# Weighted sum of shifted images: bands through DRAM, and x as the stationary operand

## The chip, the cores and the metric

The kernel runs on one core of a Trainium2 chip. The metric is device time in microseconds (us). The core has five engines that run side by side, each with its own list of instructions in order: PE (TensorE, matrix products and transposes), DVE (VectorE), ACT (ScalarE), POOL (GpSimd) and SP (SyncE, which here only issues DMA transfers). PE reads SBUF and writes PSUM, and DVE and ACT empty PSUM. Everything is float32.

## The reference

The input x has 4 images of 256 channels and 64 x 64 pixels. For each image:

```
k    = conv(x, w1, 7x7 taps, dilation 2, padding 6) + b1      # 128 channels
k    = conv(k, w2, 1x1) + b2                                  # 49 channels, one per tap
attn = softmax(k over the 49 taps)
y[c, h, w] = sum over taps (u, v) of attn[u*7+v, h, w] * xpad[c, h + 2u, w + 2v]
```

Then y is whitened: within each group of 64 channels its mean and covariance over all images and pixels are taken, five Newton-Schulz steps give the inverse square root of the covariance, that matrix is applied to the centred y, and a gain and a shift follow.

## The kernel before

Dilation 2 makes each image fall into 4 parity sub-images of 32 x 32 pixels in which the taps are dense. So there are 16 sub-images (`NSUB`), numbered n. A sub-image has 8 chunks (`NCH`) of 128 pixels, each chunk 4 rows of 32. x is held in SBUF as one tile per image and row parity, [128 channels, 2 channel halves, 32 rows, 64 columns]. A sub-image takes every second column of such a tile. Two tiles are held at a time, and `load_x` fetches the next ones during the run.

The two convolutions are one: w1 and w2 are multiplied ahead (L147) to `wf`, 49 outputs per tap. `conv_piece` (L193) issues for each of 49 taps and 2 channel halves two matmuls (L208), one for the upper 16 rows of the sub-image (written to partitions 0 to 48) and one for the lower 16 (partitions 64 to 112). That is 196 matmuls for each sub-image. Rows that a tap takes out of the sub-image are left out, so for taps with u < 3 the upper half's matmuls are shorter, and for u > 3 the lower half's.

`softmax` (L218) adds the bias on ACT (L222), transposes the logits so that a pixel has its 49 values in its partition (L227), takes the maximum, subtracts, and writes the exponentials to `e_abs` with four ACT instructions (L241), each row of a chunk at its own place. The sum and its reciprocal follow on DVE (L243, L247).

For each chunk g, `build_band` (L263) makes the 128 pixels' rows of a banded matrix over the source pixels of the chunks before, at and after it, with seven `copy_predicated` instructions on DVE (L271). `transpose_band` turns it by up to three transposes (L284), and ACT copies the result to SBUF (L291). `transpose_x` makes pixels-by-channels blocks of x (L258, L260). `weighted_sum` (L294) multiplies with the band as the stationary operand and x as the moving one, 256 columns, two or three times for each chunk (L299):

```
nc.tensor.matmul(t[:, :C], a[:, d * P : (d + 1) * P], xT[g + d - 1],
                 start=(d == ds_[0]), stop=(d == ds_[-1]))
```

DVE scales by the reciprocal and subtracts a pivot (L316). `collect` (L325) adds the result's second moments to `sig` (L333, 129 columns, the last a column of ones) and transposes it back to channels by pixels (L336); ACT copies that to the tile `y` of the image (L338).

The order is written out in a loop over chunks: a piece of the next sub-image's conv (an eighth, 24 or 26 matmuls), then x transposes of chunk g+1, the band transposes of g, the weighted sum of g-1, the collection of g-2, and at the end of a sub-image the softmax of the next. A framework sets the semaphores and may move instructions a little against the written order. Tiles named `tp` come from four PSUM tiles used in turn.

At the end stand the whitening matrices (L375 to L437, a chain of small products between PE and DVE) and the last loop (L442): 64 matmuls of 512 columns (L449), each followed by a scaling on ACT or DVE in turn, in place, and 16 stores of 1 MB.

Of the kernel before, what the change touches and what calls it, by code (L numbers as in the profile page):

```python
# [9 lines left out]
I32 = mybir.dt.int32  # L10
# [6 lines left out]
def kernel(  # L17
# [11 lines left out]
    """Dilated 7x7 conv -> 1x1 conv -> softmax over the 49 taps -> weighted sum of  # L29
    the 49 dilated shifts of x -> group whitening (Newton-Schulz) -> affine.  # L30

    Dilation 2 splits an image into 4 parity sub-images of 32x32 in which the taps
    are dense. The two convs are one conv with the weight product (49 outputs, two
    half sub-images side by side in the array's columns). The weighted sum is a
    product with a banded matrix A[source pixel, pixel] that is built per 128
    pixels (4 sub-rows) from the softmax.
    """
# [9 lines left out]
    NCH = SH * SW // P  # L47
    CR = P // SW
    NB = CR + KS - 1
# [7 lines left out]

    const = ctx.enter_context(tc.tile_pool(name="const", bufs=1))
    xpool = ctx.enter_context(tc.tile_pool(name="xp", bufs=2))
    xtpool = ctx.enter_context(tc.tile_pool(name="xtp", bufs=5))  # L60
    work = ctx.enter_context(tc.tile_pool(name="work", bufs=2))
    ps_cv = ctx.enter_context(tc.tile_pool(name="ps_cv", bufs=2, space=bass.MemoryType.PSUM))
    ps_tp = ctx.enter_context(tc.tile_pool(name="ps_tp", bufs=4, space=bass.MemoryType.PSUM))
# [6 lines left out]
    xtiles = {}  # L70

    def load_x(k):
        b, pr = divmod(k, 2)
        t = xpool.tile([P, NCC, SH, W], F32, tag="x", name=f"x_{k}")
        for cc in range(NCC):
            src = x[b, cc * P : (cc + 1) * P].rearrange("c (r two) w -> c r two w", two=2)
            nc.sync.dma_start(t[:, cc], src[:, :, pr, :])
        xtiles[k] = t

# [1 line left out]
    ident = const.tile([P, P], F32, name="ident")  # L81
    make_identity(nc, ident)
    ones = const.tile([P, P], F32, name="ones")
    nc.gpsimd.memset(ones, 1.0)
# [5 lines left out]
    # diag[p, R + w] = 1 where w is the sub-column of pixel p; mask[p, v, w'] = 1  # L90
    # where tap column v takes pixel p to source column w'
# [5 lines left out]
    mask = const.tile([P, KS, SW], I32, name="mask")  # L97
    for v in range(KS):
        nc.vector.tensor_copy(mask[:, v, :], diag[:, KS - 1 - v : KS - 1 - v + SW])

# [28 lines left out]
    with tc.tile_pool(name="w1p", bufs=1) as w1p:  # L129
# [8 lines left out]
        load_x(0)  # L138
        load_x(1)
        TG = 10  # L140
        n = 0
        for cc in range(NCC):
            for t0 in range(0, KT, TG):
# [15 lines left out]
                n += 1  # L159

    ypool = ctx.enter_context(tc.tile_pool(name="yp", bufs=1))
    y = [ypool.tile([P, NCC, H, W], F32, name=f"y_{b}") for b in range(B)]

    # Tiles whose zeros (or ones) stay where they are over the whole run.
    logit = const.tile([P, HALF * SW], F32, name="logit")
    nc.gpsimd.memset(logit, 0.0)
    NE = 2
    e_abs = []
    for k in range(NE):
        et = const.tile([P, NCH, NB, KS], F32, name=f"e_abs{k}")  # L170
        nc.gpsimd.memset(et, 0.0)
        e_abs.append(et)
    NA = 2
    at_buf = []
    for k in range(NA):
        a = const.tile([P, 3 * CR, SW], F32, name=f"at{k}")
        nc.gpsimd.memset(a, 0.0)
        at_buf.append(a)
    NY = 3
# [5 lines left out]
    pivot = const.tile([P, C], F32, name="pivot")  # L185

    sig = [ps_sg.tile([P, P + 1], F32, name=f"sig{cc}") for cc in range(NCC)]

# [4 lines left out]
    def conv_piece(n, part, parts):  # L193
        """Part of the conv of sub-image n: rows of half h in partitions 64 h."""
        k, pc = divmod(n, 2)
        xt = xtiles[k]
# [19 lines left out]
    rsum = {}  # L216

    def softmax(n):  # L218
# [7 lines left out]
        for i in range(NI):  # L226
# [7 lines left out]
        d = work.tile([P, NI, 2, KT], F32, tag="d", name=f"d_{n}", bufs=1)  # L234
        nc.vector.tensor_tensor(
            d, lt[:, :, :, :KT], mx.unsqueeze(3).to_broadcast([P, NI, 2, KT]), ALU.subtract
        )
        e = e_abs[n % NE].rearrange("p (h i) a v -> p i h (a v)", h=2)
        for j in range(CR):
            q = slice(j * SW, (j + 1) * SW)  # L240
            nc.scalar.activation(e[q, :, :, j * KS : j * KS + KT], d[q], AF.Exp)  # L241
        s = work.tile([P, NCH], F32, tag="s", name=f"s_{n}")
        nc.vector.tensor_reduce(  # L243
            s, e_abs[n % NE].rearrange("p i a v -> p i (a v)"), AX.X, ALU.add
        )
        rs = work.tile([P, NCH], F32, tag="rs", name=f"rs_{n}", bufs=3)
        nc.vector.reciprocal(rs, s)  # L247
        rsum[n] = rs

    xT = {}  # L250

    def transpose_x(g):
        n, i = divmod(g, NCH)
        k, pc = divmod(n, 2)
        t = tp()
        for cc in range(NCC):
            src = xtiles[k][:, cc, i * CR : (i + 1) * CR, bass.ds(pc, SW, 2)]
            nc.tensor.transpose(t[:, cc * P : (cc + 1) * P], src, ident)  # L258
        xt = xtpool.tile([P, C], F32, tag="xT", name=f"xT_{g}")
        nc.scalar.copy(xt, t[:, :C])  # L260
        xT[g] = xt

    def build_band(g):  # L263
        """Transposed band of chunk g: row p holds the softmax terms of pixel p at
        its source pixels, over the source rows of chunks i-1, i, i+1."""
        n, i = divmod(g, NCH)
        a = at_buf[g % NA]
        e = e_abs[n % NE]
        shape = [P, NB, SW]
        for v in range(KS):  # L270
            nc.vector.copy_predicated(  # L271
                a[:, 1 : 1 + NB, :],
                mask[:, v, :].unsqueeze(1).to_broadcast(shape),
                e[:, i, :, v].unsqueeze(2).to_broadcast(shape),
            )

    bands = {}

    def transpose_band(g):
        i = g % NCH  # L280
        ds_ = [d for d in range(3) if 0 <= i + d - 1 < NCH]
        t = tp()
        for d in ds_:
            nc.tensor.transpose(  # L284
                t[:, d * P : (d + 1) * P],
                at_buf[g % NA][:, d * CR : (d + 1) * CR, :].rearrange("p r w -> p (r w)"),
                ident,
            )
        a = work.tile([P, 3 * P], F32, tag="band", name=f"band_{g}")
        cs = slice(ds_[0] * P, (ds_[-1] + 1) * P)  # L290
        nc.scalar.copy(a[:, cs], t[:, cs])  # L291
        bands[g] = (a, ds_)

    def weighted_sum(g):  # L294
        n, i = divmod(g, NCH)
        a, ds_ = bands.pop(g)
        t = tp()
        for d in ds_:
            nc.tensor.matmul(  # L299
                t[:, :C],  # L300
                a[:, d * P : (d + 1) * P],
                xT[g + d - 1],
                start=(d == ds_[0]),
                stop=(d == ds_[-1]),
            )
        xT.pop(g - 1, None)
# [43 lines left out]
    for g in range(NG + 2):  # L350
        n, i = divmod(g, NCH)
        if g < NG and n + 1 < NSUB:
            conv_piece(n + 1, i, NCH)
# [87 lines left out]
    n = 0  # L441
# [50 lines left out]
```

## Time and profile before

| | |
|---|---|
| median of 3 runs | 1907.37 us (1906.34 to 1908.09) |
| span of the profiled execution | 1905.9 us (first to last instruction; the page gives no other time of it) |
| granted PE clock, mean | 0.980 |
| softmax of sub-image 2 to softmax of sub-image 3 (L227) | 254.57 to 362.57 us |
| conv of the first sub-image ends | 148.1 us |
| conv of the last sub-image ends | 1764.1 us |
| first matmul of whitening (L380) | 1804.04 us |
| first matmul of the last loop (L449) | 1842.80 us |

A line of a timeline or of a group names the engine, the source line, the operation, the tiles (output <- inputs) and the shape, and "x" the number of records. PEld is PE's loading of the stationary operand, which overlaps the products. A float32 matmul leaves two records, a transpose one. Ends of matmuls are modelled and overlap, so the spacing of starts tells the cost. A line of a stretch has the busy time of PE, PEld, DVE, ACT and POOL, each with its number of records, then the granted PE clock, the share of DMA time and the GB/s. A DMA line has the number of issues, the size of each, and the median time from issue to landing in us.

### The profile page before, as it was taken

How to read it: one execution, taken by the hardware profiler on the slowest of the kernel's cores; microseconds unless marked ns; L12 is line 12 of the kernel's file. 1: busy time of each engine (PE TensorE's matmuls, PEld its weight loads, DVE VectorE, ACT ScalarE, POOL GpSimd, SP SyncE). 2: the span in 40 equal slices, each digit the busy share in tenths (PEclk: the TensorE clock that was granted, in tenths of full speed). 3: DMA queues.
4: the chain of work that ended last, by engine and by line, in shares of the span. 5: the costliest groups of instructions: out<-in, count | busy, mean ns of one | idle time of the engine just before them, and what ended most of it. 6: DMA issues, size and time to landing. Idle time of an engine off the chain costs nothing.

```text
span 1905.9 us, 20030 instructions
## 1 busy us (share of the span) xinstructions
PE 1859.7 (98%) x8809; PEld 941.5 (49%) x8809; DVE 562.4 (30%) x1204; ACT 243.1 (13%) x649; POOL 4.7 (0%) x21
## 2 busy tenths in 40 slices
PE   7999999999999999999999999999999999999678
PEld 6544454444545454444554545444544444454543
DVE  0004232322324232322323323231423323231734
ACT  0001010101001010101111111101111111110314
POOL 0000000000000000000000000000000000000000
PEclk9899999999999999999999999999999999999869
DMA  8000000200020000200011000200002000000017
GB/s 224 1 0 1 1 1 1 45 0 1 1 38 7 1 0 1 45 1 1 1 23 22 1 1 1 45 0 1 1 9 37 1 0 1 1 1 1 1 53 300
DMA packets 69358, 41.29 MB, mean 22 GB/s; under 512 B 66919, under 2 KB 66968, under 8 KB 66968
## 3 DMA queue, kind: packets, MB, share of 16 engines
q1 hardware_dynamic: 68984, 33.58, 7.3%
q10 hardware_dynamic: 288, 6.42, 0.8%
q8 instruction: 70, 1.15, 0.3%
q14 instruction: 16, 0.13, 0.0%
HBM read 23.23 MB, written 16.78 MB: 21 GB/s over the span
## 4 chain that ended last, share of the span: by engine, by line
PE 97%; DVE 2%; DMA 1%; issue 0%; ACT 0%; SPq 0%
PE cv L208 73%; PE tp L299 8%; PE tp L449 3%; PE sig L333 3%; PE tp L258 3%; PE tp L147 2%; PE tp L284 2%; PE tp L336 1%; DVE at L271 1%; DMA b_sb<-in_L_conv_b_dram 1%; PE tp L414 0%; PE tp L410 0%; PE tp L406 0%; PE tp L227 0%; DVE P L417 0%
## 5 line engine op out<-in xcount | busy, mean ns | idle before, releaser
L208 PE MATMUL cv<-x,wf 128*49 128x480 f32 (+14 forms) x6272 | 1401.9, 580 | 0.0
L208 PEld LDWEIGHTS cv<-x,wf 128*49 128x49 f32 x6272 | 556.9, 123 | 752.3 <-issue 652.2
L271 DVE COPY_PREDICATED at<-mask,e_abs 128x320 f32<-128x320 int32 x896 | 444.1, 519 | 725.9 <-PE tp L284 709.5
L260 ACT COPY xT<-tp 128x256 f32<-128x256 f32 x128 | 47.4, 370 | 1086.0 <-PE tp L258 1086.0
L299 PE MATMUL tp<-xT,band 128*128 128x256 f32 x704 | 175.1, 383 | 0.0
L316 DVE SCALAR_TENSOR_TENSOR yt<-tp,rs,pivot 128x256 f32<-128x256 f32 x128 | 60.9, 476 | 366.9 <-PE tp L299 366.8
L299 PEld LDWEIGHTS tp<-xT,band 128*128 128x128 f32 x704 | 124.8, 192 | 12.2 <-ACT y L338 0.4
L333 PE MATMUL sig<-yt 128*128 128x129 f32 x512 | 92.1, 276 | 0.1
L258 PEld LDWEIGHTS tp<-ident,x 128*128 128x128 f32 x256 | 40.6, 207 | 101.6 <-issue 101.6
L333 PEld LDWEIGHTS sig<-yt 128*128 128x128 f32 x512 | 87.1, 192 | 7.0 <-DVE yt L316 0.5
L338 ACT COPY y<-tp 128x128 f32<-128x128 f32 x256 | 56.6, 278 | 159.1 <-PE tp L336 159.1
L284 PE MATMUL tp<-ident,at 128*128 128x128 f32 x352 | 60.1, 275 | 11.3 <-DVE at L271 11.3
L336 PE MATMUL tp<-ident,yt 128*128 128x128 f32 x256 | 69.5, 274 | 0.0
L258 PE MATMUL tp<-ident,x 128*128 128x128 f32 x256 | 64.1, 332 | 0.0
L291 ACT COPY band<-tp 128x384 f32<-128x384 f32 (+1 forms) x128 | 57.8, 451 | 15.4 <-PE tp L284 13.6
L449 PE MATMUL tp<-y,P 128*128 128x512 f32 x128 | 57.5, 612 | 0.0
L222 ACT ACTIVATE logit<-cv,bias 49x512 f32<-49x512 f32 x32 | 21.8, 682 | 252.3 <-PE cv L208 251.9
L284 PEld LDWEIGHTS tp<-ident,at 128*128 128x128 f32 x352 | 43.9, 146 | 12.4 <-issue 12.4
L147 PEld LDWEIGHTS tp<-w2T,w 128*128 128x128 f32 x196 | 43.2, 313 | 1.0 <-issue 1.0
L147 PE MATMUL tp<-w2T,w 128*128 128x49 f32 x196 | 43.4, 418 | 0.0
L449 PEld LDWEIGHTS tp<-y,P 128*128 128x128 f32 x128 | 25.2, 198 | 31.5 <-issue 31.5
L233 DVE TENSOR_REDUCE mx<-tp 128x8 f32<-128x392 f32 x16 | 9.1, 566 | 99.7 <-PE tp L227 99.7
(77 smaller groups left out, 236.5 us busy)
## 6 DMA issues: line engine op xcount, KB each, us to landing
x<-in_x_dram SPq DMA_DIRECT2D x16, 1024.0 KB, 11.2
out_dram<-y SPq DMA_DIRECT2D x16, 1024.0 KB, 3.8
w<-in_L_conv_w_dram ACTq DMA_DIRECT2D x2, 3136.0 KB
gain_sb<-in_L_conv_weight_dram SPq DMA_DIRECT2D x2, 0.5 KB, 17.9
shift_sb<-in_L_conv_bias_dram SPq DMA_DIRECT2D x2, 0.5 KB, 17.6
b_sb<-in_L_conv_b_dram SPq DMA_DIRECT2D x2, 0.2 KB
w_sb<-in_L_conv_w_dram SPq DMA_DIRECT2D x1, 24.5 KB
b_sb<-in_L_conv_b_dram SPq DMA_DIRECT2D x1, 0.5 KB
```

The costliest lines, as they stand in the source:

```text
L147: nc.tensor.matmul(t[:, k * KT : (k + 1) * KT], w1_sb[cc][:, :, t0 + k], w2T[:, :KT], start=True, stop=True,)
L208: nc.tensor.matmul(ps[h * HB : h * HB + KT, r0 - h * HALF : r1 - h * HALF, c0:c1], wf[:, cc, u * KS + v, :], xt[:, cc, r0 + du : r1 + du, ...
L258: nc.tensor.transpose(t[:, cc * P : (cc + 1) * P], src, ident)
L271: nc.vector.copy_predicated(a[:, 1 : 1 + NB, :], mask[:, v, :].unsqueeze(1).to_broadcast(shape), e[:, i, :, v].unsqueeze(2).to_broadcast(s ...
L284: nc.tensor.transpose(t[:, d * P : (d + 1) * P], at_buf[g % NA][:, d * CR : (d + 1) * CR, :].rearrange("p r w -> p (r w)"), ident,)
L291: nc.scalar.copy(a[:, cs], t[:, cs])
L299: nc.tensor.matmul(t[:, :C], a[:, d * P : (d + 1) * P], xT[g + d - 1], start=(d == ds_[0]), stop=(d == ds_[-1]),)
L316: nc.vector.scalar_tensor_tensor(yt_buf[g % NY][:, :, :P], t[:, :C].rearrange("p (a c) -> p a c", a=NCC), r, pivot.rearrange("p (a c) -> p ...
L333: nc.tensor.matmul(sig[cc], yt[:, cc, :P], yt[:, cc, :], start=(g == 0), stop=(g == last))
L336: nc.tensor.transpose(t[:, cc * P : (cc + 1) * P], yt[:, cc, :P], ident)
L338: nc.scalar.copy(y[b][:, cc, bass.ds(2 * i * CR + pr, CR, 2), bass.ds(pc, SW, 2)], t[:, cc * P : (cc + 1) * P].rearrange("p (r w) -> p r w ...
L449: nc.tensor.matmul(t, wm[cc], yf[:, k : k + NT], start=True, stop=True)
```

## The change

The band of a whole sub-image is now made at once by a copy through DRAM. DVE writes the normalised softmax values to a tile `zt`, at the same place in every partition and with zeros around them. SP stores it to DRAM with a row pitch of ZL+1 and loads it back with a pitch of ZL, so that each partition's values come back shifted by its own number. The masked reciprocal `rm` removes taps that leave the row.

The weighted sum goes by source block in place of by chunk: `make_block(n, m)` transposes block m of x and the band's rows that touch it; x's block is the stationary operand and the band the moving one, and the products of up to three blocks add up in a PSUM tile of a half sub-image, channels by pixels. As a block reaches 3 rows over its edges, the rows that are new and those that were written before are separate matmuls. The result, minus a pivot, is written by ACT into x's own tile in place of the sub-image's x, so the separate `y` tiles go. All eight x tiles are loaded at the start, the last six behind the product of w1 and w2. `collect` then transposes y to pixels by channels, copies it on DVE, and adds the second moments. The last loop writes to three buffers of 512 KB in place of working in place, with 32 stores. `ps_tp` has three tiles in place of four, and the y product has one pair of PSUM banks. The numbers of lines below are not those of the kernel before.

```diff
+    dram = ctx.enter_context(tc.tile_pool(name="dram", bufs=2, space=bass.MemoryType.DRAM))
-    ps_tp = ctx.enter_context(tc.tile_pool(name="ps_tp", bufs=4, space=bass.MemoryType.PSUM))
+    ps_tp = ctx.enter_context(tc.tile_pool(name="ps_tp", bufs=3, space=bass.MemoryType.PSUM))
+    ps_y = ctx.enter_context(tc.tile_pool(name="ps_y", bufs=1, space=bass.MemoryType.PSUM))
...
+    for k in range(2, 2 * B):
+        load_x(x27, k)
+    nc.vector.tensor_reduce(
+        pivot, slots[0].rearrange("p a r w -> p a (r w)")[:, :, :npix], AX.X, ALU.add
+    )
...
 def softmax(n):   # after the maximum is subtracted
+        nc.scalar.activation(d, d, AF.Exp)
+        nc.vector.tensor_reduce(s, d, AX.X, ALU.add)
+        nc.vector.reciprocal(s, s)
+        nc.vector.tensor_tensor(rm, s.unsqueeze(2).to_broadcast([P, NCH, KS]),
+            cmask.unsqueeze(1).to_broadcast([P, NCH, KS]), ALU.mult)
+        nc.vector.tensor_tensor(
+            zt[:, P : P + NCH * BR * SW].rearrange("p (i a w) -> p i a w", i=NCH, w=SW)[
+                :, :, :KS, :KS],
+            d.rearrange("p i (u v) -> p i u v", u=KS),
+            rm.unsqueeze(2).to_broadcast([P, NCH, KS, KS]), ALU.mult)
+        skew = dram.tile([P * (ZL + 1)], F32, tag="skew", name=f"skew_{n}")
+        nc.sync.dma_start(skew.rearrange("(p l) -> p l", l=ZL + 1)[:, :ZL], zt)
+        src = skew[: P * ZL].rearrange("(p l) -> p l", l=ZL)
+        nc.sync.dma_start(
+            band[:, : (NCH - 1) * BP, :].rearrange("p (i a) w -> p i (a w)", a=BP)[
+                :, :, : BR * SW],
+            src[:, z0 : z0 + n7].rearrange("p (i f) -> p i f", f=BR * SW))
+        nc.sync.dma_start(band[...last rows...], src[:, z0 + n7 : z0 + n7 + (BR - R) * SW])
...
+    def make_block(n, m):
+        t = tp()
+        for cc in range(NCC):
+            nc.tensor.transpose(t[:, cc * P : (cc + 1) * P],
+                xt[:, cc, CR * m : CR * (m + 1), bass.ds(pc, SW, 2)], ident)
+        nc.scalar.copy(xb, t[:, :C])
+        t = tp()
+        for i in range(i0, min(NCH, m + 2)):
+            a0 = BP * i + CR * (m - i) + R
+            nc.tensor.transpose(t[:, (i - i0) * P : (i - i0 + 1) * P],
+                band[:, a0 : a0 + CR, :].rearrange("p r w -> p (r w)"), ident)
+        nc.vector.tensor_copy(bb[:, :nw], t[:, b0 : b0 + nw])
+    def weighted_sum(n, half, m):
+        for cc in range(NCC):
+            for q0, q1 in ((r0, done), (done, r1)):
+                if q0 < q1:
+                    nc.tensor.matmul(
+                        ps[:, cc, q0 - half * HALF : q1 - half * HALF, :],
+                        xb[:, cc * P : (cc + 1) * P],
+                        bb[:, (q0 - w0) * SW : (q1 - w0) * SW],
+                        start=(m == first), stop=(m == last), skip_group_check=True)
+    def store_y(n, half):
+        for cc in range(NCC):
+            nc.scalar.activation(
+                yt[:, cc, half * HALF : (half + 1) * HALF, bass.ds(pc, SW, 2)],
+                ps[:, cc], AF.Identity, bias=pivot[:, cc : cc + 1])
+    def collect(n, half):
+        for i in range(half * NCH // 2, (half + 1) * NCH // 2):
+            t = tp()
+            for cc in range(NCC):
+                nc.tensor.transpose(t[:, cc * P : (cc + 1) * P],
+                    yt[:, cc, CR * i : CR * (i + 1), bass.ds(pc, SW, 2)], ident)
+            yb = yt_buf[count[0] % NY]      # NY = 2; L369 is the copy below
+            nc.vector.tensor_copy(yb[:, :, :P], t[:, :C].rearrange("p (a c) -> p a c", a=NCC))
+            for cc in range(NCC):
+                nc.tensor.matmul(sig[:, cc], yb[:, cc, :P], yb[:, cc, :], ...)
...
+    for n in range(NSUB + 1):
+        steps = [      # mb = make_block, ws = weighted_sum of sub-image n
+            [lambda: collect(n - 1, 1)] if n else [],
+            [mb(0), mb(1)],
+            [ws(0, 0), mb(2), ws(0, 1), mb(3)],
+            [ws(0, 2), mb(4), ws(0, 3), mb(5), ws(0, 4), lambda: store_y(n, 0)],
+            [mb(6), ws(1, 3), ws(1, 4)],
+            [mb(7), ws(1, 5), ws(1, 6)],
+            [lambda: collect(n, 0)],
+            [ws(1, 7), lambda: store_y(n, 1)],
+        ]
+        for part, do in enumerate(steps):
+            if on and n + 1 < NSUB:
+                conv_piece(n + 1, part, NCH)
+            ...
+            for f in do:
+                f()
+        if n + 1 < NSUB:
+            softmax(n + 1)
...
 # last loop
+                st = ring.tile([P, TR, 2, W], F32, tag="out", name=f"out_{b}_{cc}_{q}", bufs=3)
+                for pr in range(2):
+                    nc.tensor.matmul(t, wm[cc], slots[2 * b + pr][:, cc, q * TR : (q + 1) * TR, :]...)
+                    # scaled by ACT (even) or DVE (odd) into st[:, :, pr, :]
+                nc.sync.dma_start(out[b, cc * P : (cc + 1) * P, 2 * q * TR : 2 * (q + 1) * TR, :],
+                    st.rearrange("p r two w -> p (r two) w"))
```

## The prediction

> **What bounds the kernel now.** I read the page's shares first, then the chain of waits, then stretches of one sub-image each, then PE's timeline inside one stretch.
>
> ```profile
> PE 1859.7 (98%) x8809; PEld 941.5 (49%) x8809; DVE 562.4 (30%) x1204; ACT 243.1 (13%) x649; POOL 4.7 (0%) x21
> ...
> PEclk9899999999999999999999999999999999999869
> ...
> PE 97%; DVE 2%; DMA 1%; issue 0%; ACT 0%; SPq 0%
> ```
>
> PE is the chain; DVE, which loses most work by this change, is 2% of it. So only what PE issues, and what makes PE wait, counts.
>
> ```profile
> 254.57:362.57 108.00, 108.00 (x529) 53.63 (x528) 32.40 (x69) 13.30 (x38) 0.00 (x0) 1.00 0.12 20
> 362.57:470.57 108.00, 108.00 (x529) 53.59 (x528) 32.41 (x69) 13.31 (x38) 0.00 (x0) 1.00 0.00 1
> ```
>
> Each line is one sub-image from softmax to softmax: 108.00 us, PE never idle, granted clock 1.00. The first holds a 2 MB load (DMA share 0.12), the second none: traffic in the background costs PE nothing.
>
> ```profile
> 1158.23 11.56 PE L208 MATMUL cv<-x,wf 128*49 128x480 f32 x52
> 1169.72 0.51 PE L258 MATMUL tp<-ident,x 128*128 128x128 f32 x2
> 1170.06 0.49 PE L284 MATMUL tp<-ident,at 128*128 128x128 f32 x3
> 1170.39 1.46 PE L299 MATMUL tp<-xT,band 128*128 128x256 f32 x6
> 1171.69 0.39 PE L333 MATMUL sig<-yt 128*128 128x129 f32 x2
> 1171.91 0.27 PE L336 MATMUL tp<-ident,yt 128*128 128x128 f32 x1
> ...
> 1172.24 0.27 PE L336 MATMUL tp<-ident,yt 128*128 128x128 f32 x1
> 1172.44 10.67 PE L208 MATMUL cv<-x,wf 128*49 128x496 f32 x48
> ```
>
> Prices are start to start, since ends overlap. A float32 matmul leaves two records, a transpose one. A weighted-sum record of 256 columns costs 1.30/6 = 0.217 us, a sig record of 129 columns 0.11, a transpose 0.11. The first two transposes behind a conv run cost 0.34. The first conv record comes 0.20 after the last transpose. Conv records come in pairs, one for each half of the array's columns: 48 records, 24 pair steps, in 10.61 us, 0.44 a step.
>
> ```profile
> 157.83 0.50 PE L258 MATMUL tp<-ident,x 128*128 128x128 f32 x2
> 158.26 2.28 PE L208 MATMUL cv<-x,wf 128*49 128x390 f32 x10
> 160.47 0.44 PE L284 MATMUL tp<-ident,at 128*128 128x128 f32 x2
> ...
> 171.36 0.99 PE L208 MATMUL cv<-x,wf 128*49 128x434 f32 x2
> 172.28 0.70 PE L314 MATMUL tp<-first,ones 128*128 128x256 f32 x2
> ```
>
> In the head conv runs are cut at odd places. One conv matmul alone (2 records) takes 0.92 us to the next matmul (which may itself wait a little on DVE), where inside a run two records take 0.44. Ten records, 3 matmuls of one half and 2 of the other, take 2.21, about the longer half's six passes at 0.35. A run lasts as long as its longer half.
>
> **The change, part by part.** The conv matmuls themselves stay (196 a sub-image, 6272 records). PE's list for one sub-image of the changed kernel, as it is built (number = instructions, T = transposes, S = sig matmuls, ws = weighted-sum matmuls):
>
> ```
> cv24 ws2 T5 ws4 T5 | cv26 ws4 T5 ws4 T5 ws2 | cv24 T5 ws6 | cv24 T4 ws8 |
> cv24 T6 | cv1 S4 T2 S2 | cv2 S2 | cv23 ws4 | cv1 T4(softmax) |
> cv23 T6 | cv1 S4 T2 S2 | cv2 S2 | cv21 T9
> ```
>
> 1. *DVE's copy_predicated, e_abs, three of four exps, the sums with pivot, ACT's y copies: out.* Their cover was PE; worth 0 in steady state. If the cover were gone they would be worth at most the DVE share of the chain, 2%. The DVE copies that come (bands, y) and ACT's store of y are no more than went.
>
> 2. *Weighted sum, x stationary.* Before: 22 matmuls x 2 records x 0.217 = 9.5 us. After: 34 matmuls, 68 records. Per channel half and pass: one of 224 columns, six of 192, five of 128, three of 96, two of 32. Between the 129- and 256-column rows the slope is 0.83 ns a column: 0.189 + 6 x 0.163 + 5 x 0.11 = 1.72. The five shortest have no row with a 128-column stationary tile at full clock. By columns alone they cost 0.31 together (total 8.1 us); at the record of w1 x w2 (98 matmuls of 49 columns in 21.55 us, 0.22 a record) 1.1 (total 11.3). I take 0.11 each, nearest the 129-column row: 2.27 x 4 = 9.1. Change -0.4, bounds -1.4 and +1.8.
> The Trainium skill's page "TensorE: Matmul & The Clock Gate" (section LDWEIGHTS) speaks against such short pieces: a load is paid by its columns, columns/1.2 ns, an estimated 107 ns for 128 however few columns move. The trace has softmax transposes with 128 stationary and 113 moving columns at 0.12 or less (four in 0.48 us), so it doesn't contradict; by the page the sum would be 9.0, as here, and by columns alone 1.0 lower.
>
> 3. *Conv runs cut more often.* 13 runs in place of 8. A cut costs 0.11 behind the run (0.34 against 0.23 for two transposes elsewhere), 0.09 ahead, about 0.1 inside: 0.3. Five more: +1.5, bounds +1.0 and +2.5.
>
> 4. *Lone halves.* "cv1" ahead of the softmax transposes is one half alone, 512 columns, two passes: 0.87. "cv1" in the collection at the start of a sub-image: two passes of the shorter half at 0.35, 0.70, while the longer half sets the pace of that part. In the later collection the lone half is the longer one and its partners catch up: 0. Sum +1.6, bounds +0.8 and +2.4.
>
> 5. *Waits.* Collection now transposes, copies on DVE, then multiplies. From the first transpose (t = 0): six T to 0.82; DVE copies at 0.53 to 0.98 and to 1.48 (0.31 from a transpose's start to its reader, 0.45 a copy); cv1 covers to 1.6; four S to 2.5; two T; the third copy waits for its buffer (two, L369) until the first S are done, ends 2.8, S starts 2.9: 0.1 lost. cv2 covers the fourth. Behind these S wait conv matmuls and nothing else. make_block(1)'s band transposes wait 0.15 for ACT to empty one of three PSUM tiles. Softmax transposes: logit is 0.13 + 2 x 0.68 = 1.5 after conv, and PE has ws and cv1 until 2.0: 0. The second half's weighted sum waits for store_y (one buffer), 5 us of conv ahead: 0. Sum +0.35, bounds 0 and +2.
>
> 6. *Transposes.* Counts equal; the 16 of y now read every second element, as x's do (0.12 against 0.11): +0.2.
>
> 7. *The copy through DRAM.* SP's queue carries nothing else in steady state. zt is ready some 4 us behind the softmax transposes; PE then has cv23, a collection and cv21, 25 us, before the band is wanted: 21 us of cover. Write 1.38 MB, read 1.15 MB.
>
> ```profile
> x<-in_x_dram SPq DMA_DIRECT2D x16, 1024.0 KB, 11.2
> out_dram<-y SPq DMA_DIRECT2D x16, 1024.0 KB, 3.8
> ```
>
> By the stores 1.38 x 3.8 + 1.15 x 3.8 = 9.6 us; by the x loads (256-byte runs) 28. Runs here are 10.8 KB and 1.3 KB, nearer the stores: 10, hidden. At 28 it would show by 7 in each sub-image.
>
> 8. *Head.* All x is loaded behind w1: 12 MB, by 2 MB in 11.2 us about 67 us, from 61 to 128; conv of the first sub-image ends at 148. Hidden; bounds 0 and +10. The first sub-image has no earlier collection: its change is +0.6 in place of a full one.
>
> 9. *Tail.* The last sub-image has no conv. Before, conv's end (1764.1) to whitening (1804.0) is 40. After: band at 6 (softmax) + 10 (copy) = 16, against 12.4 before; then blocks and sums 13 (the first 4 us of them at half clock, as before), two waits for store_y 2.7, collections 8: 40. Change 0, bounds -4 and +8. Stores of 512 KB, three buffers: a buffer is wanted again after 3 x 1.72 = 5.2 us; written, issued and landed it takes 0.8 + 0.9 + 2.6 = 4.3, the last from halving the moving part of 3.8. Hidden; the last store lands 1.2 earlier: -1.2. If not hidden, up to +10.
>
> **Sum.** Per sub-image -0.4 + 1.5 + 1.6 + 0.35 + 0.2 = +3.2; fourteen of them +45, the first +0.6, tail and stores -1.2: +44. The profiled span is 1905.9, 1.5 below the median of the runs (1907.4); no other time of that execution is shown, so I take the 1.5 as what lies around it: 1905.9 + 44 + 1.5 = 1951.
>
> **Rivals.**
> *A, not slower: cut conv runs are free.* Conv uses 49 of 128 array columns; if a lone half ran beside its neighbours, terms 3 and 4 would vanish, leaving -0.4 + 0.55, about +0.15 a sub-image, +2, less 1.2: 1908, and 1893 with term 2 at its low end. Against: the lone matmul's 0.92 and the 2.21 for ten records. It decides once a cut costs under 0.05 us and a lone half nothing. Chance 0.11.
> *B, collection stalls.* If each S group waited for a full transpose, copy and release (1.1 us, covered 0.3), 8 x 0.8 = 6.4 more a sub-image: +96, 2047. For: two y buffers, three PSUM tiles. Against: conv halves stand in those gaps. Chance 0.08, together with milder forms above 1985.
> *C, the copy shows.* Round trip 28 us: 15 x 7 + 18 in the tail: 2074. It decides above 21 us. Against: run lengths. Chance 0.04.
> The forecast, terms 1 to 9 within their bounds: 0.77.
>
> **How the numbers follow.** The low ends of terms 2 to 6 sum to +0.6 a sub-image, +8 in all, the high ends to +8.9, +125; not all lie at one end. Half of that spread reaches 1914 to 1985 and is the forecast's own range. The range given is 1912 to 1988, leaving out most of A, B and C, about 2 in 10. A measurement of this kernel tells about 0.2% (4 us) from no change: faster 0.06 and same 0.06 (A, and a corner of the forecast), slower 0.88.
>
> **What would show it.** Right: stretches from softmax to softmax of about 111 us, PE still 100% at clock 1.00, and in them lone conv records of 0.7 to 0.9 us. Weighted-sum records of 32 columns at 0.11 start to start. Wrong: stretches of 108 (A), idle PE ahead of sig naming DVE's yt copy (B), idle PE ahead of the band transposes naming DMA (C), idle ACT in the last 60 us naming the stores.

## The result, and the profile after

The changed kernel takes 1954.4 us (median of 4 runs, 1953.86 to 1954.69), the kernel before 1907.18 (4 runs): a ratio of 1.0249, 95% interval 1.0234 to 1.0263. The forecast was 1951. The profiled execution has a span of 1952.8 us, 46.8 more than before (1952.77 against 1905.94 in the two traces).

The page's shares, and PE's granted clock and the chain by engine:

```profile
PE 1903.7 (97%) x9191; PEld 953.5 (49%) x9191; DVE 201.9 (10%) x468; ACT 150.2 (8%) x281; POOL 7.0 (0%) x17
...
PEclk9799999999999999999999999999999999999869
...
PE 96%; DMA 1%; DVE 1%; SPq 1%; ACT 0%; issue 0%; ACTq 0%; DVEq 0%
```

DVE's busy time fell by 360 us and ACT's by 93, and the time rose: PE is still the chain, and PE's busy time rose by 44.0. Two stretches from softmax to softmax:

```profile
366.90:478.18 111.28, 111.22 (x551) 54.28 (x550) 9.62 (x22) 7.47 (x16) 0.00 (x0) 1.00 0.07 24
1034.68:1145.96 111.28, 111.22 (x552) 54.31 (x551) 9.63 (x22) 7.49 (x16) 0.00 (x0) 1.00 0.07 24
```

A sub-image takes 111.28 us in place of 108.00, with PE busy for all but 0.06 of it and at clock 1.00. So the loss is not a wait that the profile names. It lies in what PE's records cost. PE's timeline from one softmax on:

```profile
1032.44 1.28 PE L336 MATMUL y<-bb,xb 128*128 128x192 f32 x8
1033.65 1.10 PE L220 MATMUL cv<-x,wf 128*49 128x512 f32 x2
1034.68 0.61 PE L238 MATMUL tp<-ident,logit 113*128 113x113 f32 x4
1035.22 10.83 PE L220 MATMUL cv<-x,wf 128*49 128x512 f32 x46
1045.98 0.98 PE L363 MATMUL tp<-ident,x 128*128 128x128 f32 x6
1046.89 0.90 PE L220 MATMUL cv<-x,wf 128*49 128x390 f32 x2
1047.72 1.16 PE L373 MATMUL sig<-yt 128*128 128x129 f32 x8
1048.71 0.40 PE L363 MATMUL tp<-ident,x 128*128 128x128 f32 x2
1048.95 0.71 PE L373 MATMUL sig<-yt 128*128 128x129 f32 x4
1049.59 1.05 PE L220 MATMUL cv<-x,wf 128*49 128x480 f32 x4
1050.58 0.71 PE L373 MATMUL sig<-yt 128*128 128x129 f32 x4
```

The two lone conv halves in these lines (two records each) take 1.03 and 0.83 us from start to start, where two records inside a run take 0.44. Around them the collection of half a sub-image cuts conv three times.

The whole span divides as follows (differences of starts in both traces; the forecast's terms beside them):

| part | before | after | change | forecast |
|---|---|---|---|---|
| start to the first softmax | 148.12 | 150.74 | +2.62 | 0 |
| first sub-image | 106.45 | 104.89 | -1.57 | +0.6 |
| the next 14 | 1512.02 | 1557.31 | +45.3 | +45 |
| last softmax to the end | 139.35 | 139.84 | +0.49 | -1.2 |

### The profile page after: what moved, and what is told of

Its sections match the earlier page's. It is cut to its first block, busy times and chain, and to the rows that moved or that the text cites. A ratio compares the mean times of both kernels' runs of the same rounds, so it can differ in the third digit from the quotient of the medians.

```text
span 1952.8 us, 19754 instructions
## 1 busy us (share of the span) xinstructions
PE 1903.7 (97%) x9191; PEld 953.5 (49%) x9191; DVE 201.9 (10%) x468; ACT 150.2 (8%) x281; POOL 7.0 (0%) x17
## 4 chain that ended last, share of the span: by engine, by line
PE 96%; DMA 1%; DVE 1%; SPq 1%; ACT 0%; issue 0%; ACTq 0%; DVEq 0%
PE cv L220 73%; PE y L336 8%; PE sig L373 4%; PE tp L490 3%; PE tp L309 2%; PE tp L298 2%; PE tp L363 2%; PE tp L155 2%; DMA w<-in_L_conv_w_dram 1%; SPq L117 1%; PE tp L238 0%; PE tp L455 0%; PE tp L451 0%; PE tp L447 0%; DMA band<-skew 0%; ACT xb L304 0%
## 5 line engine op out<-in xcount | busy, mean ns | idle before, releaser
L220 PE MATMUL cv<-x,wf 128*49 128x480 f32 (+13 forms) x6272 | 1437.4, 580 | 0.0
L336 PEld LDWEIGHTS y<-bb,xb 128*128 128x128 f32 x1088 | 154.5, 192 | 38.3 <-issue 38.2
L336 PE MATMUL y<-bb,xb 128*128 128x192 f32 (+4 forms) x1088 | 170.2, 301 | 0.0
L317 DVE COPY bb<-tp 128x320 f32<-128x320 f32 (+1 forms) x128 | 59.7, 467 | 966.7 <-PE tp L309 966.7
L304 ACT COPY xb<-tp 128x256 f32<-128x256 f32 x128 | 47.5, 372 | 1128.4 <-PE tp L298 1114.5
L369 DVE COPY yt<-tp 128x256 f32<-128x256 f32 x128 | 51.5, 423 | 353.7 <-PE tp L363 315.9
L309 PE MATMUL tp<-ident,band 128*128 128x128 f32 x352 | 61.4, 279 | 11.5 <-DMA band<-skew 10.3
L490 PE MATMUL tp<-x,P 128*128 128x512 f32 x128 | 57.0, 608 | 0.0
L309 PEld LDWEIGHTS tp<-ident,band 128*128 128x128 f32 x352 | 43.6, 146 | 14.7 <-issue 10.5
L349 ACT ACTIVATE x<-y,pivot 128x512 f32<-128x512 f32 x64 | 41.8, 707 | 12.9 <-PE y L336 12.5
```

Source lines behind the costliest of these rows:

```text
L220: nc.tensor.matmul(ps[h * HB : h * HB + KT, r0 - h * HALF : r1 - h * HALF, c0:c1], wf[:, cc, u * KS + v, :], xt[:, cc, r0 + du : r1 + du, ...
L304: nc.scalar.copy(xb, t[:, :C])
L309: nc.tensor.transpose(t[:, (i - i0) * P : (i - i0 + 1) * P], band[:, a0 : a0 + CR, :].rearrange("p r w -> p (r w)"), ident,)
L317: nc.vector.tensor_copy(bb[:, :nw], t[:, b0 : b0 + nw])
L336: nc.tensor.matmul(ps[:, cc, q0 - half * HALF : q1 - half * HALF, :], xb[:, cc * P : (cc + 1) * P], bb[:, (q0 - w0) * SW : (q1 - w0) * SW] ...
L349: nc.scalar.activation(yt[:, cc, half * HALF : (half + 1) * HALF, bass.ds(pc, SW, 2)], ps[:, cc], AF.Identity, bias=pivot[:, cc : cc + 1],)
```

## The experiments

Each run was compared with the kernel before on the same chip (its medians there: 1906.95 for the first four, 1907.63 for the next four, 1906.89 for the last two). "Per sub-image" is the time from softmax to softmax in the middle of the trace.

| kernel | median us | ratio to before, 95% interval | per sub-image | first softmax at |
|---|---|---|---|---|
| before | 1907.2 | | 108.00 | 148.1 |
| after | 1954.4 | 1.0249, 1.0234 to 1.0263 | 111.28 | 150.7 |
| before, conv runs cut in two | 1948.57 | 1.0217, 1.0202 to 1.0232 | 110.88 | 148.5 |
| before, cut behind one half | 2004.94 | 1.0515, 1.0497 to 1.0532 | 114.81 | 148.1 |
| after, collection split | 1924.79 | 1.0093, 1.0078 to 1.0108 | 109.12 | 150.4 |
| after, softmax covered by sums | 1934.13 | 1.0142, 1.0127 to 1.0157 | 109.84 | 150.5 |
| after, short sums merged | 1941.26 | 1.0176, 1.0163 to 1.0190 | 110.45 | 149.7 |
| after, DRAM copy written 3 times | 1963.97 | 1.0298, 1.0284 to 1.0312 | 111.30 | 150.4 |
| after, written 5 times | 1970.85 | 1.0335, 1.0321 to 1.0349 | 111.17 | 149.1 |
| all improvements together | 1879.14 | 0.9855, 0.9841 to 0.9868 | 106.49 | 145.0 |
| after, bias of the logits late | 1950.20 | 1.0226, 1.0211 to 1.0241 | 111.29 | 146.2 |
| four conv runs | 1872.18 | 0.9817, 0.9801 to 0.9833 | 105.83 | 146.7 |

The theory was that of the forecast: PE's stream pays for each cut of a conv run and for each half that stands alone. The rivals: cuts cost nothing (A), the collection stalls (B), the copy shows (C).

A "cut" is a place where a run of conv matmuls is interrupted by other work of PE; a "lone half" is one matmul, of one half of the sub-image, that stands without its partner between two such places.

### What a cut costs, in the kernel before

Here only the order of the kernel before is changed. Each eighth of conv is issued as two sixteenths, on both sides of the transposes, which makes 17 conv runs a sub-image in place of 8.

```diff
-            conv_piece(n + 1, i, NCH)
+            conv_piece(n + 1, 2 * i, 2 * NCH)
         if g + 1 < NG:
             transpose_x(g + 1)
         if g < NG:
             transpose_band(g)
+        if g < NG and n + 1 < NSUB:
+            conv_piece(n + 1, 2 * i + 1, 2 * NCH)
```

> The kernel before, with each eighth of the conv issued in two even parts (12 and 12 or 14 matmuls), the second between the band transposes and the weighted sum. Nothing else changes, so only the number of conv runs grows, from 8 to 17 a sub-image (the first chunk is cut once more by the order of PE's list). Theory (a cut costs 0.3 us, an even cut leaves no lone half): 9 x 0.3 = 2.7 a sub-image, 15 of them +40 us, range +25 to +60, about 1947. Rival A (cut runs are free): 0, 1907.

1948.57 us. A sub-image takes 110.88, 2.88 more for 9 more runs: 0.32 a cut. By starts, 0.13 of it lies in conv itself, 0.10 in the transposes and 0.09 in the sums. PE's timeline there:

```profile
1005.09 5.55 PE L208 MATMUL cv<-x,wf 128*49 128x480 f32 x24
1010.58 0.51 PE L258 MATMUL tp<-ident,x 128*128 128x128 f32 x2
1010.92 0.49 PE L284 MATMUL tp<-ident,at 128*128 128x128 f32 x3
1011.34 5.38 PE L208 MATMUL cv<-x,wf 128*49 128x496 f32 x24
1016.66 1.56 PE L299 MATMUL tp<-xT,band 128*128 128x256 f32 x6
```

PE is never idle in it, and no instruction is added; the two transposes behind the run take 0.34 where two take 0.23 elsewhere, and the next run starts 0.42 after the start of three, where three take 0.33 elsewhere. Rival A, which needs cuts under 0.05 us, falls. The cuts were not all even: in the first eighth PE's list leaves one half alone (two records, 1.03 us). Conv of that eighth grows by 0.25 for its two cuts, that of the other seven by 0.11 to 0.14 for one, so this half adds nothing that shows.

### What a half alone costs, in the kernel before

The same, but the transposes go behind the first matmul of each eighth, so that one half stands alone and its partner comes after them.

```diff
-    def conv_piece(n, part, parts):
+    def conv_piece(n, part, parts, between=None):
...
                 nc.tensor.matmul( ... )
+                if between:
+                    between()
+                    between = None
...
-            conv_piece(n + 1, i, NCH)
-        if g + 1 < NG:
-            transpose_x(g + 1)
-        if g < NG:
-            transpose_band(g)
+            conv_piece(n + 1, i, NCH, turn)    # turn: the two transposing steps
```

> The kernel before, with each eighth of the conv cut behind its first matmul, which is one half alone; the transposes of x and of the band stand in the cut. As many cuts as in cut_even. Theory: the cuts 2.7 a sub-image as there, and the lone halves 0.87 + 0.70 + 0.75 + 0.80 + 0.65 in the five eighths where the half left behind sets the pace, about 0 in the last three: 3.8; together 6.5, 15 sub-images +97 us, about 2004. Rival A: 0. A milder rival (cuts cost, lone halves don't): +40, as cut_even.

2004.94 us; 114.81 a sub-image, 3.93 more than with whole pairs, 0.49 in the mean of eight lone halves. PE's timeline:

```profile
1004.81 1.10 PE L208 MATMUL cv<-x,wf 128*49 128x496 f32 x2
1005.83 0.50 PE L261 MATMUL tp<-ident,x 128*128 128x128 f32 x2
1006.17 0.49 PE L287 MATMUL tp<-ident,at 128*128 128x128 f32 x3
1006.60 10.39 PE L208 MATMUL cv<-x,wf 128*49 128x496 f32 x46
```

The lone half takes 1.02 to the next start, more than two whole pair steps (0.88), though the other half's columns do nothing. The run behind it, two records shorter, gives only a part back: 1016.92 - 1006.60 = 10.32, where 48 records in pairs took 10.61. Of the rival answers, free and mildly priced, neither fits.

The mean hides what decides. Conv of each eighth of one sub-image, by starts in the traces of this run and of the one with runs cut in two (us; the last row is what was expected above, in its order):

| eighth | 1 | 2 | 3 | 4 | 5 | 6 | 7 | 8 |
|---|---|---|---|---|---|---|---|---|
| cut in two | 11.04 | 10.73 | 10.72 | 11.63 | 10.72 | 10.75 | 10.80 | 11.66 |
| cut behind one half | 11.92 | 11.41 | 11.50 | 12.46 | 11.35 | 10.86 | 10.81 | 11.69 |
| more | 0.88 | 0.68 | 0.78 | 0.83 | 0.63 | 0.11 | 0.01 | 0.03 |
| expected | 0.87 | 0.70 | 0.75 | 0.80 | 0.65 | 0 | 0 | 0 |

In the first five the half left behind is the longer one and sets the pace of the run, so the time of the lone one is lost; in the last three the lone half is the longer one, and its partners catch up.

### The collection without its cuts

`collect` is parted: all eight transposes of a half and two wide copies to SBUF go first, and the eight sig matmuls follow one conv piece later. Conv has 9 runs in place of 13; the lone half of the collection and the waits between its groups go.

```diff
-    def collect(n, half):
+    def collect_t(n, half):     # 2 PSUM tiles, 4 transposes each, 2 DVE copies
...
+    def collect_s(n, half):     # the 8 sig matmuls
...
-            [lambda: collect(n - 1, 1)] if n else [],
-            [mb(0), mb(1)],
+            [lambda: collect_t(n - 1, 1)] if n else [],
+            [lambda: collect_s(n - 1, 1) if n else None, mb(0), mb(1)],
...
-            [mb(7), ws(1, 5), ws(1, 6)],
-            [lambda: collect(n, 0)],
+            [mb(7), ws(1, 5), ws(1, 6), lambda: collect_t(n, 0)],
+            [lambda: collect_s(n, 0)],
```

> The changed kernel, with each collection in two steps: all transposes (two chunks in one PSUM tile) and two DVE copies in one step, the sig products one conv piece later. No conv matmul has to stand in a gap there: 9 conv runs a sub-image in place of 13, one lone half in place of three. Theory: -4 x 0.3 - 0.70 - 0.2 of waits = -2.1 a sub-image, about -30 us, 1924. Rival A: only the waits go, about -3 us, 1951.

1924.79 us (1922.86 to 1926.64); 2.16 less a sub-image, against the 1.2 + 0.7 + 0.2 that the forecast's own prices give. In the profiled run, the slowest of the four, the part behind the last softmax is 3.6 longer than in the changed kernel; that was not followed up. The timeline shows what is gone:

```profile
1029.60 1.22 PE L365 MATMUL tp<-ident,x 128*128 128x128 f32 x8
1030.75 10.66 PE L220 MATMUL cv<-x,wf 128*49 128x390 f32 x48
1041.35 2.06 PE L378 MATMUL sig<-yt 128*128 128x129 f32 x16
```

Transposes, a whole conv run, sig: the same records in three blocks.

### The softmax without its lone half

Step 5 is emptied: `[mb(7), ws(1, 5), ws(1, 6)]` move to step 7, so that these sums, and no conv half, stand between the end of conv and the softmax transposes. 11 runs.

```diff
-            [mb(7), ws(1, 5), ws(1, 6)],
+            [],
             [lambda: collect(n, 0)],
-            [ws(1, 7), lambda: store_y(n, 1)],
+            [mb(7), ws(1, 5), ws(1, 6), ws(1, 7), lambda: store_y(n, 1)],
```

> The changed kernel, with the last block and its weighted sums moved behind the last conv piece, so that PE has 3.9 us of other work while ACT makes the logits. The lone conv half ahead of the softmax transposes goes, with its cut, and so does one other cut. Theory: -0.87 - 2 x 0.3 = -1.5 a sub-image, 15 of them -22 us, 1932. Rival A: 0, 1954.

1934.13 us, 1.44 less a sub-image. Added up, this edit and the one before take 3.60 away, more than the 3.28 that the change had cost.

### The short sums

The rows that are new and those that were written before go in one matmul, 20 in place of 34 a sub-image, with the same columns in all.

```diff
-            for q0, q1 in ((r0, done), (done, r1)):
+            for q0, q1 in ((r0, r1),):
```

> The changed kernel, with the rows that are new and those that were written before in one weighted-sum matmul in place of two: 20 matmuls (40 records) a sub-image in place of 34 (68), the same 4736 columns. Theory (a short record costs 0.11 us at least, or what its stationary load costs): per pass and channel half 2 x (2 x 0.189 + 2 x 0.270 + 0.11) = 2.06, times 4 is 8.2, against 8.9 measured now: -0.7 a sub-image, 16 of them -11 us, 1943. Rival (paid by columns alone): 28 records of 3 ns fewer, -1 us, 1953.

1941.26 us, 0.82 less a sub-image for 28 fewer records, 0.03 a record. The mean says little here too: records of 128 columns and more save nothing when they are joined, as their columns stay. By the measured prices of the longer records, the run would save 0.87 if a record of 32 or 96 columns costs 0.11, as the forecast had it, and 0.41 if it costs what it takes to its own next start (0.056 and 0.104 in the mean; see the last section). The low and the high price of term 2 (columns alone, and 0.22 a record) both fall.

### The copy through DRAM, made longer

The store is issued 3 or 5 times, with no other edit.

```diff
-        nc.sync.dma_start(skew.rearrange("(p l) -> p l", l=ZL + 1)[:, :ZL], zt)
+        for _ in range(3):      # or 5
+            nc.sync.dma_start(skew.rearrange("(p l) -> p l", l=ZL + 1)[:, :ZL], zt)
```

> The changed kernel, with the store to DRAM done three times, one after the other, before the band is loaded: the round trip is 9.4 us longer. Theory (21 us of cover, of which 10 are used; 12.3 us are left in the trace): nothing in the steady state, 9.4 in the tail, and some 4 in the first sub-image, whose cover is shorter: +14 us, 1968. Rival C (the copy is already at the edge of its cover): 9.4 in each sub-image, +150, 2104.

> The changed kernel, with the store to DRAM done five times: the round trip is 18.8 us longer, which is more than what is left of the cover. Theory: 18.8 - 12.3 = 6.5 in each of 14 sub-images, 14 in the first, 19 in the tail: +124 us, 2078. If +20 only, the cover is longer than thought.

1963.97 and 1970.85 us. The second was a clear miss: its round trip is longer than the forecast's cover, and yet the sub-image takes 111.17, as without it. SP's queue and PE's timeline with five stores:

```profile
1035.71 19.83 SPq L273 DMA_DIRECT2D skew<-zt  x5
1059.95 0.37 SPq L277 DMA_DIRECT2D band<-skew  x1
```

```profile
1057.86 0.51 PE L299 MATMUL tp<-ident,x 128*128 128x128 f32 x2
1058.29 20.31 PE L220 MATMUL cv<-x,wf 128*49 128x434 f32 x94
1078.53 0.44 PE L310 MATMUL tp<-ident,band 128*128 128x128 f32 x2
```

The load starts 24 us after the first store. In the changed kernel the band's transposes stand right behind the first x transposes, and a conv run of 48 records follows them. Here the framework that orders PE's list has moved 94 conv records ahead of them, and the cover grew with it. The store is the only thing that was edited, so the order seems to go by how long the transfer is reckoned to take; that was not looked into. With three stores the list is already moved in part (19 conv matmuls ahead of the band's transposes). So these two kernels differ from the changed one in two things, and how much cover its own order has was not settled by them. What the changed kernel's own trace gives is 12.4 us left.

The tail has no conv to move. From the last softmax to the last sig matmul it is 39.2, 48.8 and 57.6 us with one, three and five stores, 9.6 and 18.4 more. With three stores that is the whole difference (measured +9.6). With five the medians differ by 16.5 and the traces by 16.0: 1.6 less before the first softmax, 0.6 less in the first sub-image, 1.7 less in the next 14, and 19.9 more from the last softmax to the end. Why the three are shorter is open. PE's waits for the band, in all, of the changed kernel and of the one with five stores:

```profile
PE tp L309 <- DMA band<-skew: 10.3, 1, 10.3
```

```profile
PE tp L310 <- DMA band<-skew: 29.6, 1, 29.6
```

One wait each in the whole execution, in the tail.

### The bias of the logits

In the head of the changed kernel PE stops:

```profile
14.08 0.56 PE L132 MATMUL tp<-b_sb,w2T 128*128 128x1 f32 x2 [10.75 <-DMA b_sb<-in_L_conv_b_dram]
14.50 8.97 PE L155 MATMUL tp<-w2T,w 128*128 128x49 f32 x40
25.26 12.95 PE L155 MATMUL tp<-w2T,w 128*128 128x49 f32 x58 [1.79 <-DVE bias L134]
```

The same work of the kernel before:

```profile
14.51 21.69 PE L147 MATMUL tp<-w2T,w 128*128 128x49 f32 x98
```

DVE adds b2 to a PSUM tile `tp` (L134) once b2 has landed, at 25.1. Until then DVE's copies of `wf` behind it wait, and their `tp` tiles stay full. With four tiles PE just did not run out of them; with three it waits 1.79 us. The experiment moves the small matmul and the addition behind the product of w1 and w2.

```diff
-    t = tp()
-    nc.tensor.matmul(t[:, :1], w2T, b1_sb, start=True, stop=True)
     bias = const.tile([P, 1], F32, name="bias")
-    nc.vector.tensor_tensor(bias, t[:, :1], b2_sb, ALU.add)
...
+    t = tp()     # behind the loop that fills wf
+    nc.tensor.matmul(t[:, :1], w2T, b1_sb, start=True, stop=True)
+    nc.vector.tensor_tensor(bias, t[:, :1], b2_sb, ALU.add)
```

> The changed kernel, with the logits' bias (a matmul and a DVE addition that wait for b1 and b2) behind the product of w1 and w2 in place of ahead. Theory for the head: with three PSUM tiles in place of four the wait for b2, held by DVE, stops PE 1.8 us and makes the product start late; without it the first softmax comes at 145 in place of 150.7 (145.0 in the kernel named best, which has this edit too): -5 us, 1949. Rival: the late head comes from the x loads or the clock's start, then 0, 1954.

1950.20 us. The first softmax comes at 146.15, 4.6 earlier than in the changed kernel and 2.0 earlier than before. The head of PE's timeline:

```profile
11.53 15.76 PE L152 MATMUL tp<-w2T,w 128*128 128x49 f32 x71 [7.59 <-DMA w<-in_L_conv_w_dram]
```

The stop is gone, and the products start with w1's landing at 11.5, no longer behind the small matmul that waited for b1 until 14.1. So of the 4.6, 3.0 come from the earlier start and 2.0 from the stop, less 0.4 elsewhere in the head. The stop alone, with a fourth tile and the old order, was not run.

### The improvements together

The four edits in one: collection split, sums ahead of the softmax, sums merged, bias late. The sig matmuls are placed between blocks of sums, not alone between conv runs, and conv has 7 runs.

```diff
+            [lambda: collect_t(n - 1, 1)] if n else [],
+            [mb(0), lambda: collect_s(n - 1, 1) if n else None, mb(1)],
...
+            [mb(6), ws(1, 3), ws(1, 4)],
+            [],
+            [lambda: collect_t(n, 0)],
+            [mb(7), ws(1, 5), ws(1, 6), lambda: collect_s(n, 0), ws(1, 7), lambda: store_y(n, 1)],
```

> The changed kernel with the collections in two steps, the softmax covered, the weighted-sum matmuls merged, and the bias of the logits made behind the product of w1 and w2. 7 conv runs a sub-image, no lone half, 40 weighted-sum records. Theory against the kernel before: cuts -0.3, weighted sum 8.2 against 9.5 = -1.3, strided transposes +0.2: -1.4 a sub-image, 15 of them -21, head 0, tail and first sub-image about 0: 1887, range 1878 to 1897. Rival A: the cuts and lone halves count for nothing, only the weighted sum and waits do: below 1954 by 11 to 16, about 1940.

1879.14 us, a ratio to before of 0.9855 (0.9841 to 0.9868). A stretch, and PE's timeline at its end:

```profile
359.00:465.49 106.49, 106.49 (x524) 51.64 (x522) 8.99 (x18) 7.36 (x15) 0.00 (x0) 1.00 0.07 26
```

```profile
1094.00 2.32 PE L336 MATMUL y<-bb,xb 128*128 128x320 f32 x8
1096.15 1.95 PE L378 MATMUL sig<-yt 128*128 128x129 f32 x16
1097.94 0.92 PE L336 MATMUL y<-bb,xb 128*128 128x224 f32 x4
1098.69 0.55 PE L238 MATMUL tp<-ident,logit 113*128 113x113 f32 x4
1099.18 10.86 PE L220 MATMUL cv<-x,wf 128*49 128x512 f32 x48
```

Sums, sig and softmax stand in one block. Against before, a sub-image saves 1.51: sums 0.91, transposes 0.47, conv 0.13 for one run fewer.

Then the same with everything that is not conv gathered into four blocks (the steps are shown without their lambdas and the guard for n = 0):

```diff
+            [],
+            [mb(0), mb(1), collect_t(n-1, 1), ws(0, 0), mb(2), ws(0, 1), collect_s(n-1, 1), mb(3)],
+            [],
+            [ws(0, 2), mb(4), ws(0, 3), mb(5), ws(0, 4), store_y(n, 0), mb(6)],
+            [],
+            [],
+            [ws(1, 3), ws(1, 4), ws(1, 5), collect_t(n, 0)],
+            [mb(7), ws(1, 6), collect_s(n, 0), ws(1, 7), store_y(n, 1)],
```

> The kernel named best with its conv in 4 runs a sub-image in place of 7 (48, 50, 72 and 26 matmuls), the same other work between them in a changed order. Theory: 3 cuts x 0.32 (the price that cut_even measured) = -1.0 a sub-image, 15 of them -14 us, 1865; waits between the longer stretches of other work would give some of it back. Rival (only lone halves cost): 0, 1879.

1872.18 us, a ratio to before of 0.9817 (0.9801 to 0.9833), and the fastest of all. A sub-image takes 105.83, 0.65 less for three runs fewer: 0.22 a cut, where 0.32 was carried over from the kernel before, so only half of the expected gain came. Conv gives its part (0.35 for three cuts, 0.12 each); transposes and sums give 0.30, where two thirds of a cut's price would be 0.6. The waits that the expectation named would fit, but were not shown.

## Why the prediction was right, and where its steps were not

**The mechanism.** It held: the loss is conv cut into more runs and halves that stand alone, with PE busy throughout. By kind of record, conv costs 2.23 more in a sub-image than before, the sig matmuls 0.99, the weighted sum 0.10, and the transposes 0.04 less. Conv's 2.23 are the lone halves' 1.57 (below) and five cuts at 0.13 each. The transposes of y start 0.12 apart in place of 0.11, as term 6 had it.

**The sum.** Fourteen sub-images were to cost 45 us more and cost 45.3. The price of a cut (0.3) measured 0.32 in the kernel before and 0.22 between the last two kernels; the forecast's bounds of +1.0 to +2.5 for five cuts are 0.2 to 0.5 each. The forecast's own range of 1914 to 1985 does not come out of its working: half of the spread from +8 to +125, taken to both sides of +44, gives about 1933 to 1992, which holds the result too.

**Lone halves.** Forecast 0.87, 0.70 and, in the later collection, 0. In the trace they take 1.03, 0.83 and 0.99 from start to start, but the runs beside them give some of it back. Against the same eighths of conv in the kernel before, the three places cost 1.00, 0.94 and 0.28 more in conv; less one, two and two cuts at 0.13 that is 0.87, 0.68 and 0.02. Removed with their cuts, they took 1.44 (two cuts and the softmax's half: forecast 1.5) and 2.16 (four cuts, the collection's half, its waits: 2.1).

**The weighted sum.** In the stretch its starts span 9.62 us, but about 0.7 of that is the price of the cuts around it; without it 8.93, against 9.1 forecast and 9.52 before. The sign that the forecast gave, records of 32 columns at 0.11 from start to start, did not appear as it was put: they take 0.028 or 0.112, 0.056 in the mean. Yet the price holds, as the record behind two of them starts its successor 0.08 late (last section), which makes 0.11 for each. The Trainium skill's page "TensorE: Matmul & The Clock Gate" (section LDWEIGHTS) has each load paid by its stationary columns, an estimated 107 ns for 128. The trace agrees: with that delay a short record costs 0.11, and the loads around the short records start 0.110 and 0.112 apart.

**Waits.** 0.35 was forecast. The share of `make_block(1)` was under-sized: in the changed kernel

```profile
1060.94 0.51 PE L298 MATMUL tp<-ident,x 128*128 128x128 f32 x2
1061.29 0.38 PE L309 MATMUL tp<-ident,band 128*128 128x128 f32 x2
1061.51 0.40 PE L298 MATMUL tp<-ident,x 128*128 128x128 f32 x2
1061.97 0.55 PE L309 MATMUL tp<-ident,band 128*128 128x128 f32 x3
1062.45 10.68 PE L220 MATMUL cv<-x,wf 128*49 128x434 f32 x48
```

the third and fourth groups last 0.46 and 0.48 to the next start, where such groups last 0.23 and 0.33 elsewhere, or 0.42 for the fourth ahead of a conv run: 0.29 in place of 0.15. In the collection, the four S behind the last two T take 0.64 in place of 0.44; 0.10 of it lies ahead of them, as forecast, and 0.09 is the cut behind them. Rival B's 0.8 at each of eight groups is nowhere to be seen.

**The copy.** SP's queue of the changed kernel:

```profile
1038.77 0.32 SPq L272 DMA_DIRECT2D skew<-zt  x1
1043.49 0.37 SPq L276 DMA_DIRECT2D band<-skew  x1
```

zt is ready 4.1 us behind the softmax transposes at 1034.68 (some 4 forecast); the load is issued 4.7 later and takes 5.4 in the median of its issues, so the round trip is 10.1 (10 forecast). A second, small load (112 KB, the last rows), which the forecast's 1.15 MB left out, lands 0.3 later. The band's first transposes stand at 1061.29, 12.4 us after the first load landed. Rival C falls for this kernel.

**The head failed.** Term 8 looked at the loads of x only, which indeed stay hidden, and gave 0. Of the measured +2.62, 2.04 are the first half of the product, with PE's stop on three `tp` tiles in it. The loss of one tile was weighed for `make_block` and not for the product of w1 and w2, where a DVE instruction that waits for a small load holds the tiles. The other 0.6 is conv in the head: the eight records between the two halves of the product take 3.42 us in place of 2.96, and conv behind the product 0.13 more. Behind the product the granted clock is 0.50 for the first 4.87 us before and for the first 5.38 us after, which may be the 0.13; for the eight records the traces name no cause.

**The first sub-image failed.** It was to cost +0.6 and came out at -1.57. It has no earlier half to collect: in the kernel before that is worth 1.55 against a full stretch, in the changed one 6.39, with cuts, lone half and waits. The forecast valued the difference at 2.6; it is 4.8. By kind of record, the first sub-image lies below a full one by 0.39 in conv before and by 2.87 after, by 0.89 and 2.28 in sig, by 0.78 and nothing in the sums; its transposes (with the pivot's product) cost 0.52 more before and 1.24 less after. So 2.48 of the 4.8 is conv: before, it has 10 records fewer there and saves only 0.39, as its runs are cut at odd places. The forecast showed these places (the ten records at 158.26, the lone matmul at 171.36) and did not count that they go. This is read from the traces; no run tried it by itself.

**Tail and stores.** From the last softmax to the last sig matmul 2.1 us more than before (0 forecast, bounds -4 and +8); the last loop to the end 1.5 us less (1.2 forecast), the whitening between them 0.1 less. The stores landed in the 2.6 us of the forecast:

```profile
out_dram<-out SPq DMA_DIRECT2D x32, 512.0 KB, 2.6
```

The misses of the head (+2.6), the first sub-image (-2.2) and the tail (+1.7) add up to 2.1, the steady part to 0.3; with the rounding of the sum that is how 46.8 stands beside 44. That the first two nearly cancel is luck.

## What to carry to other kernels

Where PE is the chain, read not only which instructions a change adds but where it cuts the long uniform stream: here each cut cost 0.2 to 0.3 us, and a column half left alone 0.6 to 0.9 more where the other half set the pace and about nothing where it did not, with PE shown busy throughout, and the same work gathered into few blocks turned a loss of 2.5% into a gain of 1.8%. When a pool loses a buffer, go through every user of that pool, the ones in the head first, and ask which instruction can hold its tiles while it waits for a small load. An experiment that lengthens a transfer tells of its cover only if the order of the other engines stays as it was.

## What was not expected of the hardware

A short record of the weighted sum does not show its price where it stands. These are starts of PE's records in the changed kernel, all with 128 stationary columns:

| start us | record | to the next start, us |
|---|---|---|
| 1089.462 | sum, 192 moving columns | 0.165 |
| 1089.627 | sum, 192 | 0.163 |
| 1089.790 | sum, 32 | 0.028 |
| 1089.818 | sum, 32 | 0.112 |
| 1089.930 | sum, 192 | 0.246 |
| 1090.176 | sum, 192 | 0.162 |
| 1090.338 | sum, 32 | 0.028 |
| 1090.366 | sum, 32 | 0.112 |
| 1090.478 | transpose | 0.180 |

The two short records take 0.14 together, but the record behind them takes 0.246 where 0.165 is usual, or 0.180 where a transpose takes 0.11. With that delay a pair costs 0.22, or 0.21 ahead of a transpose, so a record of 32 columns costs about 0.11. Two of 96 columns followed by one of 128 come to the same (0.085, 0.112 and then 0.139 in place of 0.110). The records of the stationary loads start 0.110 and 0.112 apart here, so the loads seem to set the pace; that is read from the trace, and the run with the sums merged, which saved 0.82 where these prices give 0.87, is the only one that bears on it. Whoever takes the time to the next start for the price of a record goes wrong where short and long records alternate.
